# Softmax totals of layer 0: from TensorE to VectorE and GpSimd, in a kernel of two attention layers

## The chip, the cores and the metric

The kernel runs on one core of a Trainium2 chip (trn2). The core has five engines with instruction queues of their own: TensorE (PE in the profile, its weight loads PEld), VectorE (DVE), ScalarE (ACT), GpSimd (POOL) and SyncE (SP, which here only issues DMAs). Each works through its queue in program order and waits on semaphores. The metric is device time in microseconds of one execution, as the median over several runs.

## The reference, cut to what matters

The input is x of 8 batches, 512 channels and 32 x 32 positions (T = 1024), in float32. Layer 0 normalizes by groups, computes q, k and v with 8 heads of 64 channels, applies softmax attention over the positions, adds, and projects. Layer 1 does a second attention that mixes heads and normalizes the attention matrix.

```python
def _L0_conv_ref(x, gn_w, gn_b, qkv_w, qkv_b, proj_w, proj_b):
    ...
    qkv = jnp.einsum('oc,bct->bot', qkv_w, normed) + qkv_b[None, :, None]
    q, k, v = jnp.split(qkv, 3, axis=1)
    ...
    weight = jnp.einsum('bct,bcs->bts', q, k)
    weight = jax.nn.softmax(weight.astype(jnp.float32), axis=-1).astype(q.dtype)
    a = jnp.einsum('bts,bcs->bct', weight, v).reshape(b, c, t)
    out = jnp.einsum('oc,bct->bot', proj_w, xf + a) + proj_b[None, :, None]
    return out.reshape(b, -1, h, w)
...
x = x + _L0_conv_ref(_gn(x), ...)
x = x + _L1_conv_ref(_gn(x), ...)
return x
```

The change concerns the denominator of layer 0's softmax: for each head and each query position t, the sum of exp(weight) over the 1024 key positions s, and its reciprocal, which scales the attention's output.

## The kernel before

The order of the work on every engine is written out by hand (a manual schedule); pools only give out the buffers. Layer 0 runs batch after batch. For one batch, `attention0` works through NI = 64 steps. A step is one chunk of 128 key positions (kc, 0 to 7) for one pair of heads (hp) and one half of the 1024 queries (f); eight steps with the same hp and f are a group g, and there are 8 groups a batch.

- `scores(i)`: four matmuls of 64 x 64 x 512 make the scores of two heads, keys on the partitions and 512 queries in the free dimension, in PSUM; ScalarE writes their exponential to a tile e[i] of 128 x 1024 (pool of 7 buffers).
- `values(i)`: four matmuls add v times e[i] to the group's accumulators; after the last chunk ScalarE copies them to u[g] (two tiles, L1127).
- `sums(i)`: VectorE adds e[i] to zacc[g], seven adds a group (L1101 the first, L1103 the others). The partitions of zacc still hold different keys.
- `totals(g)`, once for two groups: TensorE multiplies zacc with a matrix of ones, which sums over the partitions (L1135), ScalarE copies the result to `row` (L1141), and two DMAs spread it over 128 partitions as zc (L1146).
- `reciprocals(g)`: VectorE adds the two halves of u (L1150), takes the reciprocal of zc (L1153), a DMA writes it to DRAM (zd, L1155), and two DMAs read it back, repeated over 64 partitions each (rzb, L1158). Two small instructions (L1163, L1167) fill a check.
- `finish(g)`: VectorE multiplies u with rzb (L1174) and adds the result to xa (L1176).

The loop takes two steps at a time: scores of i and i + 1, then values and sums of i - 2 and i - 1, then what the agenda holds for i and i + 1. For an odd g, whose last chunk is done at step i, it holds totals at i + 2, reciprocals of both groups at i + 6, and finish at i + 10 and i + 12. What is left at the loop's end is flushed after the next batch's k projection (`qk0`), ahead of its v projection (`v0`).

The same agenda puts other work between the steps: ScalarE's start of xa (L872) and sums for the next batch's normalization (L826, L832), VectorE's channel statistics of the batch before (L652, slots 4 to 15), the combinations of weights (L772 to L778, batches 0 to 2), the small steps of the next normalization (slots 43 to 47: `means` with the matmul L626, `squares` with L637, `scale`), and on SP the loads of x (L719) and of weights (L747, slots 32 and 33). After the loop VectorE combines tiles of the next input (`combine_right`, L885 to L888), which the k projection's second part (L906) reads.

Of the kernel before, what the change touches and what calls it, by code (L numbers as in the profile page):

```python
# [9 lines left out]
F32 = mybir.dt.float32  # L10
I32 = mybir.dt.int32
AF = mybir.ActivationFunctionType
ALU = mybir.AluOpType
AX = mybir.AxisListType
# [4 lines left out]
P = 128  # L19
# [448 lines left out]
def tile_two_attention_layers(  # L468
# [19 lines left out]
    nc = tc.nc  # L488
    B, C, T = x_d.shape
# [4 lines left out]
    FB = 512  # L494
# [206 lines left out]
    with ExitStack() as l0:  # L701
# [27 lines left out]
        HC = C // 2  # L729
# [21 lines left out]
        def load_blocks(which, queue=nc.sync, tag="u0"):  # L751

            t = left_tile(which, 0)
            if tag == "junk":
                a21[which] = zpool.tile([P, T], F32, tag=tag, name=f"a21_{which}", bufs=1)[
                    :, :C
                ].rearrange("p (k o) -> p k o", k=2)
            else:
                a21[which] = zpool.tile([P, 2, HC], F32, tag=tag, name=f"a21_{which}", bufs=3)
            for dst, i, j in (  # L760
                (t[:, 0], 0, 0), (t[:, 1], 0, 1), (a21[which], 1, 0), (t[:, 2], 1, 1),
            ):
                for k in range(2):
                    queue.dma_start(
                        out=dst[:, k],
                        in_=SOURCES[which][ts(2 * j + k, P), i * HC : (i + 1) * HC],
                    )
# [307 lines left out]

        def attention0(b, agenda):
            q, k, v = q_t[b], k_t[b], v_t[b]
            e, acc, u, zacc, zc, rzb = {}, {}, {}, {}, {}, {}

            def scores(i):  # L1080

# [13 lines left out]
            def sums(i):  # L1095
                g, kc = i // NG, i % NG
                if kc == 1:
                    zacc[g] = zpool.tile(
                        [P, 2, FB], F32, tag="zacc", name=f"zacc_{b}_{g}", bufs=3
                    )  # L1100
                    nc.vector.tensor_add(zacc[g], e[i - 1], e[i])  # L1101
                elif kc > 1:
                    nc.vector.tensor_add(zacc[g], zacc[g], e[i])  # L1103

            def values(i):

                g, hp, kc = i // NG, i // NG % (H // 2), i % NG
                if kc == 0:
                    acc[g] = [
                        ps_a.tile([P, FB], F32, tag=f"a{a}", name=f"a0_{b}_{g}_{a}", bufs=2 - a)  # L1110
                        for a in range(2)
                    ]
                for a in range(2):
                    rows = slice(a * D, a * D + D)
                    for m in range(2):
                        nc.tensor.matmul(  # L1116
                            acc[g][a][m * D : m * D + D], v[rows, kc, ts(2 * hp + m, D)],
                            e[i][rows, m], start=(kc == 0), stop=(kc == NG - 1),
                        )
                if kc == NG - 1:  # L1120

                    u[g] = [
                        zpool.tile([P, FB], F32, tag=f"u{a}", name=f"u_{b}_{g}_{a}", bufs=3 - a)
                        for a in range(2)
                    ]
                    for a in (1, 0):
                        nc.scalar.copy(u[g][a], acc[g][a])  # L1127

            def totals(g):

                HB = FB // 2
                z = ps_a.tile([P, FB], F32, tag="a0", name=f"z_{b}_{g}", bufs=2)
                for i in range(2):
                    for c in range(4):
                        nc.tensor.matmul(  # L1135
                            z[c * 32 : c * 32 + 32, ts(i, HB)], ones[:, :32],
                            zacc[g - 1 + i][:, c // 2, ts(c % 2, HB)],
                            start=True, stop=True, tile_position=(0, c * 32),
                        )
                row = zpool.tile([P, FB], F32, tag="row", name=f"row0_{b}_{g}", bufs=1)  # L1140
                nc.scalar.copy(row, z)  # L1141
                for i in range(2):
                    t = zc[g - 1 + i] = stat.tile(
                        [P, T // P], F32, tag="zc", name=f"zc_{b}_{g - 1 + i}", bufs=4
                    )
                    nc.sync.dma_start(out=t, in_=row[0::32, ts(i, HB)])  # L1146

            def reciprocals(g):

                nc.vector.tensor_add(u[g][0], u[g][0], u[g][1])  # L1150
                zs = zc[g]
                rz = stat.tile([P, T // P], F32, tag="rz0", name=f"rz_{b}_{g}")
                nc.vector.reciprocal(rz, zs)  # L1153
                zd = dram.tile([2, FB], F32, tag=f"zd0_{b}_{g}", name=f"zd0_{b}_{g}")
                nc.sync.dma_start(out=zd, in_=rz)  # L1155
                rzb[g] = zpool.tile([P, FB], F32, tag="rzb", name=f"rzb_{b}_{g}")
                for m in range(2):
                    nc.sync.dma_start(  # L1158
                        out=rzb[g][m * D : m * D + D], in_=zd[m].partition_broadcast(D)
                    )  # L1160
                col = b * H + g
                junk = stat.tile([P, T // P], F32, tag="junk0", name=f"junkz_{b}_{g}")
                nc.vector.tensor_scalar(  # L1163
                    junk, zs, 1.0, 0.0, ALU.mult, ALU.add, accum_out=chk[:, 1, col : col + 1]
                )
                r2 = stat.tile([P, T // P], F32, tag="r20", name=f"r2_{b}_{g}")
                nc.vector.scalar_tensor_tensor(  # L1167
                    r2, rz, 1.0 / RZ_MAX, rz, ALU.mult, ALU.mult,
                    accum_out=chk[:, 0, col : col + 1],
                )  # L1170

            def finish(g):
                hp, f = g % (H // 2), g // (H // 2)
                nc.vector.tensor_mul(u[g][0], u[g][0], rzb[g])  # L1174
                dst = xa_t[b][:, hp, ts(f, FB)]
                nc.vector.tensor_add(dst, dst, u[g][0])  # L1176


            for i in range(0, NI + 2, 2):
                if i < NI:  # L1180
                    scores(i)
                    scores(i + 1)
                if i >= 2:
                    for w in (i - 2, i - 1):
                        values(w)
                        sums(w)
                    if (i - 1) % NG == NG - 1:
                        g = (i - 1) // NG
                        if g % 2:
                            agenda.at(i + 2, lambda g=g: totals(g))  # L1190
                            for j in range(2):
                                agenda.at(i + 6, lambda g=g - 1 + j: reciprocals(g))
                                agenda.at(i + 10 + 2 * j, lambda g=g - 1 + j: finish(g))
                agenda.run(i)
                agenda.run(i + 1)

# [927 lines left out]
```

## Time and profile before

| | us |
|---|---|
| median of 3 runs | 3935.7 (3933.7 to 3948.0) |
| the profiled execution: its own time | 3948.0 |
| its span, first to last instruction | 3946.2 |
| TensorE busy over the span | 3871.6 (98%) |
| VectorE | 2736.6 (69%) |
| ScalarE | 1966.8 (50%) |
| GpSimd | 207.4 (5%) |
| layer 0's stretch from 95 to 1750 us: TensorE busy | 1649.2 of 1655 |
| the same stretch: VectorE, ScalarE, GpSimd | 1064.1, 801.7, 0.0 |
| granted TensorE clock | 0.998 |

In the lines of groups, the columns are line, engine, operation, output and inputs by name, shapes and count, then the total busy time, the mean of one in ns, and the idle time of the engine just before them with what ended it. In the timeline they are start and length in us, engine, line, operation and count; idle time before it stands in brackets. Matmul records overlap, so the spacing of their starts says more than their length.

### The profile page before, as it was taken

To read this page: it belongs to the slowest core of one execution; us is meant where nothing else is said; L and a number is where in the kernel's file an instruction comes from. 1 tells how busy PE (TensorE), PEld (TensorE's weight loads), DVE (VectorE), ACT (ScalarE), POOL (GpSimd) and SP (SyncE) were. 2 spreads that over 40 slices of the span, in tenths; PEclk is the share of its full clock that TensorE was granted. 3 is DMA by queue.
4 is the path that set the end of the run, shared out by engine and by line. 5 is a ranking of instruction groups with operands and counts; after the bars stand their busy time and mean duration, and the time that the engine had idled before them with its cause. 6 is when DMAs were issued, how large, how long until landed. Compare 5 with 4: busy or idle time off the path is not lost. (4 is left out here: it accounts for less than half of the span.)

```text
span 3946.2 us, 95344 instructions
## 1 busy us (share of the span) xinstructions
PE 3871.6 (98%) x41868; PEld 1822.3 (46%) x41868; DVE 2736.6 (69%) x3713; ACT 1966.8 (50%) x2400; POOL 207.4 (5%) x210
## 2 busy tenths in 40 slices
PE   8999999999999999999999999999999999999998
PEld 4353535344353535344554544545545545445454
DVE  4747476665758474756867958859768678678597
ACT  1726354453627172534725717528447257176275
POOL 0000000000000000000110100201101102002010
PEclk9999999999999999999999999999999999999999
DMA  3313131212121121216947839749559479297395
GB/s 120 120 53 116 49 116 43 84 35 77 55 75 66 64 73 52 87 46 168 221 135 190 230 97 229 191 128 239 167 149 228 142 177 223 97 227 204 114 228 146
DMA packets 249593, 519.09 MB, mean 132 GB/s; under 512 B 51024, under 2 KB 58192, under 8 KB 242512
## 3 DMA queue, kind: packets, MB, share of 16 engines
q1 hardware_dynamic: 241984, 500.08, 44.7%
q0 software_dynamic: 7184, 12.81, 1.6%
q8 instruction: 331, 5.42, 0.6%
q14 instruction: 94, 0.77, 0.1%
HBM read 197.16 MB, written 46.92 MB: 62 GB/s over the span
## 5 line engine op out<-in xcount | busy, mean ns | idle before, releaser
L1712 DVE STREAM_TRANSPOSE et<-e 128x2048 f32<-128x2048 f32 x256 | 589.5, 2303 | 133.5 <-ACT e L1697 132.5
L1742 PEld LDWEIGHTS a<-et,v 128*64 128x64 f32 x16384 | 506.4, 138 | 294.0 <-issue 268.5
L1726 DVE BATCH_NORM_STATS2 bn<-e 128x6 f32<-128x512 f32 x1024 | 635.0, 680 | 0.0
L1093 ACT ACTIVATE e<-s 128x1024 f32<-128x1024 f32 x512 | 497.1, 1026 | 232.8 <-PE s L1088 232.7
L1659 ACT COPY raw<-s 128x1024 f32<-128x1024 f32 x480 | 470.2, 1018 | 218.9 <-PE s L1647 192.5
L1697 ACT ACTIVATE e<-m 128x1024 f32<-128x1024 f32 x512 | 496.2, 1021 | 157.4 <-PE m L1684 55.1
L1742 PE MATMUL a<-et,v 128*64 128x64 f32 x16384 | 554.7, 224 | 8.7 <-issue 6.2
L1103 DVE TENSOR_TENSOR zacc<-zacc,e 128x1024 f32<-128x1024 f32 x384 | 468.8, 1221 | 124.6 <-ACT e L1093 100.5
L1647 PE MATMUL s<-k,q 64*64 64x512 f32 x4096 | 515.6, 606 | 6.9 <-DVE q L1506 3.2
L1088 PE MATMUL s<-q,k 64*64 64x512 f32 x4096 | 490.3, 594 | 2.3 <-ACT e L1093 2.3
L1116 PE MATMUL a<-e,v 64*64 64x512 f32 x4096 | 484.1, 589 | 0.0
L1684 PE MATMUL m<-re,wmix 32*32 32x512 f32 x8192 | 312.8, 599 | 17.8 <-DMA re<-raw 14.4
L1116 PEld LDWEIGHTS a<-e,v 64*64 64x64 f32 x4096 | 156.6, 133 | 282.8 <-issue 282.3
L1088 PEld LDWEIGHTS s<-q,k 64*64 64x64 f32 x4096 | 146.4, 133 | 284.2 <-issue 217.8
L1647 PEld LDWEIGHTS s<-k,q 64*64 64x64 f32 x4096 | 128.0, 132 | 222.5 <-issue 90.5
L1790 POOL DMA_DIRECT2D zd<-rz x96 | 52.3, 550 | 3390.0 <-DMA y<-x 1868.5
L1466 PE MATMUL pv<-wv,y 128*128 128x512 f32 x480 | 216.0, 603 | 0.0
L1758 ACT COPY q<-a 64x256 f32<-64x256 f32 x256 | 93.8, 367 | 136.4 <-PE a L1742 134.5
L1466 PEld LDWEIGHTS pv<-wv,y 128*128 128x128 f32 x480 | 89.3, 191 | 120.9 <-issue 107.5
L1684 PEld LDWEIGHTS m<-re,wmix 32*32 32x32 f32 x8192 | 69.3, 103 | 163.2 <-ACT raw L1659 71.7
L1472 DVE COPY v<-pv 128x512 f32<-128x512 f32 x30 | 20.7, 690 | 159.7 <-ACT v L1472 80.3
L906 PE MATMUL pv_p<-left_v,tmp 128*128 128x256 f32 x512 | 115.0, 380 | 3.3 <-DVE tmp L935 3.3
(318 smaller groups left out, 3859.5 us busy)
## 6 DMA issues: line engine op xcount, KB each, us to landing
re<-raw SPq DMA_DIRECT2D x1024, 256.0 KB
left_q<-left_q SPq DMA_DIRECT2D x17, 1792.0 KB
left_p<-left_p SPq DMA_DIRECT2D x17, 1792.0 KB
left_k<-left_k SPq DMA_DIRECT2D x10, 1792.0 KB
x<-in_x_dram SPq DMA_DIRECT2D x32, 512.0 KB
rzb<-zd SPq DMA_DIRECT2D x128, 128.0 KB
x<-x SPq DMA_DIRECT2D x64, 256.0 KB
y<-x SPq DMA_DIRECT2D x32, 512.0 KB
```

The costliest lines, as they stand in the source:

```text
L1088: nc.tensor.matmul(ps[c * D : c * D + D, m], k[r, hp, k0 : k0 + D], q[r, hp, ts(f, FB)], start=True, stop=True,)
L1093: nc.scalar.activation(e[i], ps, AF.Exp, scale=S0 * S0)
L1103: nc.vector.tensor_add(zacc[g], zacc[g], e[i])
L1116: nc.tensor.matmul(acc[g][a][m * D : m * D + D], v[rows, kc, ts(2 * hp + m, D)], e[i][rows, m], start=(kc == 0), stop=(kc == NG - 1),)
L1466: nc.tensor.matmul(ps[:, m], y_t[b][:, c, ts(2 * i + m, P)], w[:, c], start=(c == 0), stop=(c == NCC - 1),)
L1647: nc.tensor.matmul(ps[c * D : c * D + D, m], qo_t[b][r, p, hp, ts(c, D)], k_t[b][r, hp, ts(kh, FB)], start=True, stop=True,)
L1659: nc.scalar.copy(dst, ps)
L1684: nc.tensor.matmul(ps[a // 2][c * 32 : c * 32 + 32, a % 2].rearrange("p (r h k) -> p h r k", r=2, h=2), wmix[rows].rearrange("p g i -> p ( ...
L1697: nc.scalar.activation(e[:, :, 2 * h : 2 * h + 2].rearrange("p r a k -> p a r k"), ps[h].rearrange("p a (r k) -> p a r k", r=2), AF.Exp,)
L1712: nc.vector.transpose(self.et[p, u].rearrange("p kb (r st a) g q -> p st kb r (a g q)", r=2, st=2)[:, st], self.e[p, s].rearrange("p r a ( ...
L1726: nc.vector.bn_stats(self.bn[n][:, p % 2, s, a], e[:, :, a].rearrange("p r k -> p k r"))
L1742: nc.tensor.matmul(acc[two * D : two * D + D, s].rearrange("p (x q) -> p x q", q=4), v_t[b][:, kb, ts(g, D)], et[:, kb, :, g], start=(kb = ...
```

## The change

`sums`: the first three chunks of each group are added by GpSimd into a new tile zpart (two instructions); VectorE starts its own sum at chunk 4 with e[3] + e[4], adds chunks 5 and 6, then zpart, then chunk 7 (five adds). `totals` is now made for every group, without TensorE and ScalarE: VectorE transposes zacc in blocks of 32 x 32 and sums runs of 32 columns, once for each head, and transposes the small result again; four DMAs bring the four partition blocks of it side by side as zc. `reciprocals` first adds these four parts, and works on 32 x 32 instead of 128 x 8. The agenda has totals at i + 2, reciprocals at i + 8 and finish at i + 12 for every group. Buffer counts: a21 and u0 2 instead of 3, zacc 2 instead of 3.

```diff
@@ -756,7 +756,7 @@
                     :, :C
                 ].rearrange("p (k o) -> p k o", k=2)
             else:
-                a21[which] = zpool.tile([P, 2, HC], F32, tag=tag, name=f"a21_{which}", bufs=3)
+                a21[which] = zpool.tile([P, 2, HC], F32, tag=tag, name=f"a21_{which}")
             for dst, i, j in (
                 (t[:, 0], 0, 0), (t[:, 1], 0, 1), (a21[which], 1, 0), (t[:, 2], 1, 1),
             ):
@@ -1075,7 +1075,7 @@
 
         def attention0(b, agenda):
             q, k, v = q_t[b], k_t[b], v_t[b]
-            e, acc, u, zacc, zc, rzb = {}, {}, {}, {}, {}, {}
+            e, acc, u, zacc, zpart, zc, rzb = {}, {}, {}, {}, {}, {}, {}
 
             def scores(i):
 
@@ -1095,12 +1095,19 @@
             def sums(i):
                 g, kc = i // NG, i % NG
                 if kc == 1:
-                    zacc[g] = zpool.tile(
-                        [P, 2, FB], F32, tag="zacc", name=f"zacc_{b}_{g}", bufs=3
+                    zpart[g] = zpool.tile(
+                        [P, 2, FB], F32, tag="zpart", name=f"zpart_{b}_{g}", bufs=1
                     )
+                    nc.gpsimd.tensor_add(zpart[g], e[i - 1], e[i])
+                elif kc == 2:
+                    nc.gpsimd.tensor_add(zpart[g], zpart[g], e[i])
+                elif kc == 4:
+                    zacc[g] = zpool.tile([P, 2, FB], F32, tag="zacc", name=f"zacc_{b}_{g}")
                     nc.vector.tensor_add(zacc[g], e[i - 1], e[i])
-                elif kc > 1:
+                elif kc > 4:
                     nc.vector.tensor_add(zacc[g], zacc[g], e[i])
+                    if kc == NG - 2:
+                        nc.vector.tensor_add(zacc[g], zacc[g], zpart[g])
 
             def values(i):
 
@@ -1120,7 +1127,7 @@
                 if kc == NG - 1:
 
                     u[g] = [
-                        zpool.tile([P, FB], F32, tag=f"u{a}", name=f"u_{b}_{g}_{a}", bufs=3 - a)
+                        zpool.tile([P, FB], F32, tag=f"u{a}", name=f"u_{b}_{g}_{a}")
                         for a in range(2)
                     ]
                     for a in (1, 0):
@@ -1128,45 +1135,43 @@
 
             def totals(g):
 
-                HB = FB // 2
-                z = ps_a.tile([P, FB], F32, tag="a0", name=f"z_{b}_{g}", bufs=2)
-                for i in range(2):
-                    for c in range(4):
-                        nc.tensor.matmul(
-                            z[c * 32 : c * 32 + 32, ts(i, HB)], ones[:, :32],
-                            zacc[g - 1 + i][:, c // 2, ts(c % 2, HB)],
-                            start=True, stop=True, tile_position=(0, c * 32),
-                        )
-                row = zpool.tile([P, FB], F32, tag="row", name=f"row0_{b}_{g}", bufs=1)
-                nc.scalar.copy(row, z)
-                for i in range(2):
-                    t = zc[g - 1 + i] = stat.tile(
-                        [P, T // P], F32, tag="zc", name=f"zc_{b}_{g - 1 + i}", bufs=4
+                HN = FB // 32
+                pz = stat.tile([P, 2, HN], F32, tag="pz", name=f"pz_{b}_{g}")
+                for m in range(2):
+                    zt = zpool.tile([P, FB], F32, tag="zt", name=f"zt_{b}_{g}_{m}", bufs=1)
+                    nc.vector.transpose(zt, zacc[g][:, m])
+                    nc.vector.reduce_sum(
+                        pz[:, m], zt.rearrange("p (n i) -> p n i", i=32), axis=AX.X
                     )
-                    nc.sync.dma_start(out=t, in_=row[0::32, ts(i, HB)])
+                pt = stat.tile([P, 32], F32, tag="pt", name=f"pt_{b}_{g}")
+                nc.vector.transpose(pt, pz.rearrange("p m n -> p (m n)"))
+                zc[g] = stat.tile([32, 4, 32], F32, tag="zc", name=f"zc_{b}_{g}")
+                for c in range(4):
+                    nc.sync.dma_start(out=zc[g][:, c], in_=pt[c * 32 : c * 32 + 32])
 
             def reciprocals(g):
 
                 nc.vector.tensor_add(u[g][0], u[g][0], u[g][1])
-                zs = zc[g]
-                rz = stat.tile([P, T // P], F32, tag="rz0", name=f"rz_{b}_{g}")
+                zs = stat.tile([32, 32], F32, tag="zs0", name=f"zs_{b}_{g}")
+                nc.vector.reduce_sum(zs, zc[g].rearrange("p c j -> p j c"), axis=AX.X)
+                rz = stat.tile([32, 32], F32, tag="rz0", name=f"rz_{b}_{g}")
                 nc.vector.reciprocal(rz, zs)
                 zd = dram.tile([2, FB], F32, tag=f"zd0_{b}_{g}", name=f"zd0_{b}_{g}")
-                nc.sync.dma_start(out=zd, in_=rz)
+                nc.sync.dma_start(out=zd.rearrange("m (n j) -> (m n) j", j=32), in_=rz)
                 rzb[g] = zpool.tile([P, FB], F32, tag="rzb", name=f"rzb_{b}_{g}")
                 for m in range(2):
                     nc.sync.dma_start(
                         out=rzb[g][m * D : m * D + D], in_=zd[m].partition_broadcast(D)
                     )
                 col = b * H + g
-                junk = stat.tile([P, T // P], F32, tag="junk0", name=f"junkz_{b}_{g}")
+                junk = stat.tile([32, 32], F32, tag="junk0", name=f"junkz_{b}_{g}")
                 nc.vector.tensor_scalar(
-                    junk, zs, 1.0, 0.0, ALU.mult, ALU.add, accum_out=chk[:, 1, col : col + 1]
+                    junk, zs, 1.0, 0.0, ALU.mult, ALU.add, accum_out=chk[:32, 1, col : col + 1]
                 )
-                r2 = stat.tile([P, T // P], F32, tag="r20", name=f"r2_{b}_{g}")
+                r2 = stat.tile([32, 32], F32, tag="r20", name=f"r2_{b}_{g}")
                 nc.vector.scalar_tensor_tensor(
                     r2, rz, 1.0 / RZ_MAX, rz, ALU.mult, ALU.mult,
-                    accum_out=chk[:, 0, col : col + 1],
+                    accum_out=chk[:32, 0, col : col + 1],
                 )
 
             def finish(g):
@@ -1186,11 +1191,9 @@
                         sums(w)
                     if (i - 1) % NG == NG - 1:
                         g = (i - 1) // NG
-                        if g % 2:
-                            agenda.at(i + 2, lambda g=g: totals(g))
-                            for j in range(2):
-                                agenda.at(i + 6, lambda g=g - 1 + j: reciprocals(g))
-                                agenda.at(i + 10 + 2 * j, lambda g=g - 1 + j: finish(g))
+                        agenda.at(i + 2, lambda g=g: totals(g))
+                        agenda.at(i + 8, lambda g=g: reciprocals(g))
+                        agenda.at(i + 12, lambda g=g: finish(g))
                 agenda.run(i)
                 agenda.run(i + 1)
```

## The prediction

> **What bounds the kernel now.** I read the page's busy shares, then the windows of one batch of layer 0, its timeline, the groups by line and the waits. Over the attention loop of batch 1 (columns: stretch, its length, busy time of PE, PEld, DVE, ACT, POOL with instruction counts, clock, DMA share, GB/s):
>
> ```profile
> 310.50:420.50 110.00, 109.71 (x1036) 38.16 (x1036) 89.47 (x146) 86.09 (x104) 0.00 (x0) 1.00 0.29 101
> ```
>
> TensorE has no idle time (0.3 us); VectorE is next with 89.5 of 110 us; GpSimd does nothing. So a microsecond taken from TensorE is a microsecond gained, as long as VectorE, which serves it in program order, keeps up. The timeline around one totals step:
>
> ```profile
> 342.19 1.07 PE L1135 MATMUL z<-zacc,ones 128*32 128x256 f32 x16
> 343.19 1.95 PE L1088 MATMUL s<-q,k 64*64 64x512 f32 x16
> 343.33 0.59 ACT L1141 COPY row<-z 128x512 f32<-128x512 f32 x1 [1.52 <-PE z L1135]
> ```
>
> The totals hold TensorE for 1.0 us. Two such steps with nothing special between them start 28.64 us apart (129.01 and 157.65). Without a totals step the loop advances by one block of 16 records (two chunks' scores, or values) in 1.716 us (starts at 348.39, 350.11, 351.83, 353.54), so 16 blocks are 27.46 us and the totals cost up to 1.18 us. I take 1.1 us. A group (8 key chunks) lasts 8 x 1.716 = 13.73 us without totals.
>
> **What the change takes from TensorE.** Each batch has four totals steps, three inside the loop and one behind the next batch's k projection. Three in the loop: 3 x 1.1 = 3.3 us a batch. ScalarE's row copy goes too (0.59 us each), worth nothing on the path: ScalarE is busy 86 of 110 us and waits for scores. The PSUM buffer of z is no wait today (0.6 us in all before L1116 that another engine ended), and the smaller buffer counts for u, zacc and a21 add none: in the changed order each is freed a group or more before its reuse.
>
> **What VectorE gets.** The rows, from the groups by line:
>
> ```profile
> L1103 DVE TENSOR_TENSOR zacc<-zacc,e 128x1024 f32<-128x1024 f32 x384 | 468.8, 1221 | 124.6 <-ACT e L1093 100.5 <-DVE zacc L1103 1.4 <-ACT row L1141 0.5
> L1712 DVE STREAM_TRANSPOSE et<-e 128x2048 f32<-128x2048 f32 x256 | 589.5, 2303 | 133.5 <-ACT e L1697 132.5
> L566 DVE TENSOR_REDUCE sel<-ident 128x32 f32<-128x128 f32 x1 | 0.4, 359 | 0.0
> L1829 POOL TENSOR_TENSOR q<-q,rzb 128x1024 f32<-128x1024 f32 x24 | 56.6, 2358 | 165.5 <-DMA rzb<-zd 130.9 <-ACT raw L1659 19.7 <-PE a L1742 8.2
> L1366 POOL TENSOR_TENSOR right<-y 128x1024 f32<-128x1024 f32 x14 | 34.0, 2431 | 58.5 <-ACT e L1697 35.1 <-DMA re<-raw 23.4
> ```
>
> Per group: two of seven adds leave, -2 x 1.22 = -2.44 us. Two transpositions of 128x512 come: a quarter of 2303 is 0.58 (lower bound); adds of 1024 and 512 columns (1221 and 685 ns) show a fixed part near 0.15, which gives 0.69 (taken). Two run sums of 128x512: the nearest row of that width, the 128x512 statistics at 680 ns, gives 0.68 (taken); the small reductions (128x72 in 208, 128x128 in 280 ns) extend to 0.78. The last transposition is a small operation, 0.17. Together 2.91. The reciprocals get one reduction of exactly the form of L566 (0.36) and a 32-wide reciprocal (L1784: 320 ns against 197). So about +1.0 us a group: batch 1 would go from 89.5 to some 95 us, with one more reciprocals step inside the loop, of 106.7. Still under the period; but the order matters more than the sum.
>
> **The chain.** In the changed VectorE order one group reads: five adds (L1106, L1108, L1110), reciprocals of the group before (u add, zs, rz), this group's totals, finish of the group before (waits for rzb), then the next five adds. Today adds lie between reciprocals and finish and cover the way of rz to DRAM and back; there the adds of the first chunks have gone to GpSimd, and only the totals cover. The length of that way, quiet, behind the k projection:
>
> ```profile
> 451.81 0.20 DVE L1153 RECIPROCAL rz<-zc 128x8 f32<-128x8 f32 x1 [2.14 <-DMA zc<-row]
> 452.04 0.32 SPq L1155 DMA_DIRECT2D zd<-rz  x1
> 453.44 1.13 SPq L1158 DMA_DIRECT2D rzb<-zd  x2
> 457.01 0.69 DVE L1174 TENSOR_TENSOR u<-u,rzb 128x512 f32<-128x512 f32 x1 [3.86 <-DMA rzb<-zd]
> ...
> 462.26 1.21 DVE L935 TENSOR_TENSOR tmp<-tmp,pv_p 128x1024 f32<-128x1024 f32 x1
> ...
> 463.53 1.35 PE L906 MATMUL pv_p<-left_v,tmp 128*128 128x256 f32 x5 [0.24 <-DVE tmp L935]
> ```
>
> 5.0 us from the end of rz to the multiplication; beside weight transfers up to 8.2 (1631.08 to 1639.29). I take 5.0. The totals (four dependent steps of 0.69 + 0.1, then 0.2: 3.4 us) fit inside it. Adds that depend on one another start 1.33 us apart:
>
> ```profile
> 361.38 5.21 DVE L1103 TENSOR_TENSOR zacc<-zacc,e 128x1024 f32<-128x1024 f32 x4
> ```
>
> (5.21 - 1.22) / 3. The chain of a group is thus finish 1.34 (355.91 to 357.25), adds 4 x 1.33 + 1.14 = 6.46, u add 0.61, zs and rz 0.36 + 0.32 + 0.1, DMA 5.0: 14.2 us against TensorE's 13.73. VectorE falls behind by 0.45 us with each finish; six lie in the loop.
>
> **GpSimd beside VectorE.** The two adds take 2.36 to 2.43 us each and start when chunks 1 and 2 are ready. Their result is wanted at chunk 6, some 5 us after they can be done, and e has 7 buffers, which lets an add be about 8 us late before an exponential waits. So GpSimd itself is covered; with the cover gone it would cost what exceeds 8 us. What no row shows is a VectorE instruction with two SBUF inputs beside a GpSimd one. What is shown is one input:
>
> ```profile
> 1976.29 2.44 POOL L1366 TENSOR_TENSOR right<-y 128x1024 f32<-128x1024 f32 x1 [8.19 <-DMA re<-raw]
> 1977.39 2.30 DVE L1712 STREAM_TRANSPOSE et<-e 128x2048 f32<-128x2048 f32 x1
> ```
>
> 2.30 us is the transposition's usual time. Bounds of the cost: 0, and both adds in the chain's way, 4.8 us a group. The second add mostly falls in the totals, which are one-input work like this row; the first begins when the last adds and the u add are due, and an instruction that meets a 2.4 us add at a random point would wait 1.2. I take 1.2 us a group. The Trainium skill (SBUF — State Buffer, section "Who interferes with whom") speaks against the change: a VectorE instruction with two SBUF inputs and a GpSimd one that reads SBUF exclude each other, the later one waiting out the whole instruction; by that the price would lie between 2.4 and 4.8 us a group, and the sum below at +130 to +245 us. No run here shows it yet.
>
> **Sum for a batch.** Lateness of VectorE: 1.0 from the first groups (four channel statistics of 1.4 us each fall between their adds; my estimate, 0.5 to 2), 6 x (0.45 + 1.2) = 9.9, and 2.9 for the normalization's small steps, which lie between adds (388.26 to 388.92, and 391.38 to 394.54, less 0.95 of slack before chunk 6): 13.8 us. TensorE pays it at its own in-order points: the matmul that waits for gs_m (L626, now behind a totals step on VectorE), a late e, and the k projection, whose cover is:
>
> ```profile
> 425.76 1.23 DVE L886 TENSOR_TENSOR tmp<-n,tmp 128x1024 f32<-128x1024 f32 x1
> 430.95 1.45 PE L906 MATMUL pk_p<-tmp,left_k 128*128 128x512 f32 x3
> ```
>
> 4.0 us between them today, less 1.8 for the reciprocals now ahead of L885: 2.2. Stall 13.8 - 2.2 = 11.6 us. Behind the k projection z's 1.1 us go, but the last group's totals follow L962 on VectorE: from 449.07, totals 3.4, four DMA issues 0.6 apart and 1.85 to land 3.65, zs and rz 0.8, DMA 5.0, finish 1.34: 463.2, against 462.26 today, and TensorE already waits there (0.24). Net +0.8. Each group's other zc DMAs have 8 us until they are read; SP has no other work then, except a weight load ahead of some.
>
> Per batch 11.6 - 3.3 + 0.8 = +9.1 us, times 8 = **+73 us**. The profiled execution took 3948.0 (span 3946.2 and 1.8 around it), 12.3 over the median of the runs; on the median, 3935.7 + 73 = **4009 us**. Layer 1 is unchanged and keeps its time.
>
> **Rivals.** (A) Both GpSimd adds stand in the chain: 6 x 5.25 + 3.9 - 2.2 - 3.3 + 0.8 = +30.7 a batch, 4181. For it: late VectorE adds drift into GpSimd's time; against: the totals leave GpSimd a free stretch. (B) No cost beside GpSimd: 6 x 0.45 + 3.9 - 2.2 - 2.5 = +1.9 a batch, 3951. For it: the undisturbed transposition. (C) The other side, faster: the way to DRAM and back gets shorter, since rz leaves as 32 packets of 128 bytes where 128 of 32 go today. From 4.5 us on the chain is under 13.73, VectorE recovers, and the saving of 3.3 less 0.8 stays: -20 us, 3916, or 3909 if the end of the batch keeps pace too. Against it: most of the 5.0 us are two landings, not packets. That the change does not do what it says I can exclude: in the changed order the z rows are gone and each group has two GpSimd adds.
>
> **How the numbers follow.** Forecast 0.40, own range 3980 to 4066 (0.6 to 2.4 us a group beside GpSimd); A 0.17, B 0.23, C 0.20. About 0.5%, 20 us, is what a measurement of this kernel tells from no change. C gives 0.15 faster and 0.05 same; B 0.02, 0.13 and 0.08 slower; the rest is slower: 0.17, 0.18, 0.65. The range reaches from inside C (3912) to A at three quarters of its price (6 x 4.05: +188, 4124).
>
> **What would show it.** L1179 (u times rzb) idle for rzb in most groups, about 1 to 2 us; L1108 longer than 1.23 us or idle while a GpSimd add runs; TensorE idle before L626 and in the k projection by DVE, about 90 us in layer 0; layer 1 equal within 5 us. Wrong if TensorE stays without gaps in the loop (then C), or if VectorE's adds stay at 1.22 us with no idle time beside GpSimd (then B).

## The result, and the profile after

| | before | after |
|---|---|---|
| median, same chip (6 runs each) | 3941.1 us | 4089.0 us |
| ratio, 95% interval | | 1.0377 (1.0365 to 1.039) |
| span of the profiled execution | 3946.2 | 4092.9 |
| first transposition of layer 1 (a mark for the end of layer 0) | 1832.6 | 1985.8 |
| from there to the end of the span | 2113.6 | 2107.1 |

The change costs 147.9 us, twice the 73 forecast and outside the forecast's own range (3980 to 4066), and all of it lies in layer 0: its end comes 153.2 us later, and what follows is 6.5 us shorter.

The page of after, its line of busy time and its row of granted clocks (tenths of full speed, 40 slices):

```profile
PE 3883.7 (95%) x41356; PEld 1824.4 (45%) x41356; DVE 2975.7 (73%) x3969; ACT 1950.9 (48%) x2368; POOL 557.0 (14%) x338
...
PEclk9999898999999999999999999999999999999999
```

TensorE is busy for 12 us more than before although the totals' matmuls (34.3 us of rows at L1135) are gone: some of its matmuls have become slower (the part on the prediction has their lines). The windows of after show the attention loop of batch 1 (the stretch that took 110.00 us before) and what lies inside it:

```profile
322.50:456.50 134.00, 118.57 (x1036) 40.13 (x1034) 120.36 (x175) 86.47 (x102) 44.93 (x16) 0.95 0.26 90
...
400.00:412.00 12.00, 4.15 (x40) 1.22 (x32) 11.37 (x15) 3.26 (x5) 5.00 (x2) 0.88 0.34 136
412.00:420.00 8.00, 3.73 (x18) 1.55 (x22) 6.12 (x15) 1.02 (x1) 1.05 (x1) 0.50 0.12 38
```

The loop now takes 134 us, and VectorE (third figure) is busy for 120.4 us of it, more than TensorE: 89.5 before, some 95 in the forecast. In the middle of it TensorE stands still for 12 us and then runs at a granted clock of 0.50. What it waited for in layer 0 (waits of after: line, what ended them, total us, times, longest):

```profile
PE pm L626 <- DVE gs_m L624: 81.9, 7, 12.8
PE pk_p L906 <- DVE tmp L886: 24.8, 7, 3.6
PE pv_p L906 <- DVE tmp L935: 15.8, 7, 3.2
PE s L1088 <- ACT e L1093: 8.6, 13, 2.8
```

All waits of TensorE from 90 to 1870 us add up to 143.3 us (5.8 before, from 90 to 1760 us), and 122.5 of them are the first three places, those at which it needs something from VectorE. So VectorE is late; its timeline over one group of after, and GpSimd's, show why:

```profile
389.32 1.23 DVE L1110 TENSOR_TENSOR zacc<-zacc,zpart 128x1024 f32<-128x1024 f32 x1
390.65 1.23 DVE L1108 TENSOR_TENSOR zacc<-zacc,e 128x1024 f32<-128x1024 f32 x1
391.80 2.86 DVE L1154 TENSOR_TENSOR u<-u,u 128x512 f32<-128x512 f32 x1
394.58 0.36 DVE L1156 TENSOR_REDUCE zs<-zc 32x32 f32<-32x128 f32 x1
394.98 0.34 DVE L1158 RECIPROCAL rz<-zs 32x32 f32<-32x32 f32 x1
395.25 0.12 DVE L1168 TENSOR_SCALAR_CACHE_REDUCE junkz<-zs 32x32 f32<-32x32 f32 x1
...
395.35 1.59 DVE L1172 SCALAR_TENSOR_TENSOR r<-rz 32x32 f32<-32x32 f32 x1
...
400.23 0.69 DVE L1179 TENSOR_TENSOR u<-u,rzb 128x512 f32<-128x512 f32 x1 [0.22 <-DMA rzb<-zd]
```

```profile
390.69 3.42 POOL L1101 TENSOR_TENSOR zpart<-e,e 128x1024 f32<-128x1024 f32 x1 [10.03 <-DVE zacc L1110]
394.19 2.71 POOL L1103 TENSOR_TENSOR zpart<-zpart,e 128x1024 f32<-128x1024 f32 x1
```

GpSimd's first add is released when VectorE has read zpart (L1110) and starts beside an add of VectorE, which keeps its 1.23 us; GpSimd's takes 3.42 instead of 2.37. The u add of VectorE (L1154), issued next, takes 2.86 us where it took 0.69, and ends at 394.66, 0.55 us after GpSimd's first add (394.11): it looks like a wait for that add, and then the u add's own work. The reductions and the reciprocal beside the second one are not lengthened, but the check with two inputs (L1172), 0.17 us before, takes 1.59 and ends with it (396.9). A long instruction on a page of times can thus be a wait that no wait view shows. The groups of layer 0 say that this is the rule. The u add and the check of before, then the groups of after:

```profile
L1150 DVE TENSOR_TENSOR u<-u,u 128x512 f32<-128x512 f32 x64 | 43.9, 685 | 0.0
L1167 DVE SCALAR_TENSOR_TENSOR r<-rz 128x8 f32<-128x8 f32 x64 | 10.7, 167 | 0.0
```

```profile
L1154 DVE TENSOR_TENSOR u<-u,u 128x512 f32<-128x512 f32 x64 | 134.7, 2105 | 0.0
L1142 DVE STREAM_TRANSPOSE zt<-zacc 128x512 f32<-128x512 f32 x128 | 90.2, 704 | 2.5
L1143 DVE TENSOR_REDUCE pz<-zt 128x16 f32<-128x512 f32 x128 | 87.8, 686 | 4.4
L1172 DVE SCALAR_TENSOR_TENSOR r<-rz 32x32 f32<-32x32 f32 x64 | 77.8, 1216 | 0.0
```

The u add means 2105 ns (685 before), the check 1216 (167 before): (1.42 + 1.05) x 64 = 158 us of VectorE's time. The single u adds leave nothing between: 42 of the 64 start while a GpSimd add runs and last 2.83 to 2.86 us, whether that add was issued 0.1 or 1.2 us earlier; the other 22 meet none and last 0.68 to 0.69. From one finish to the next (384.01, 400.23, 416.32 us) a group takes 16.2 us on VectorE, against TensorE's 13.73.

### The profile page after: what moved, and what is told of

It reads as the page before. It is cut to its first block, busy times and chain, and to the rows that moved or that the text cites. A ratio compares the mean times of both kernels' runs of the same rounds, so it can differ in the third digit from the quotient of the medians.

```text
span 4092.9 us, 95103 instructions
## 1 busy us (share of the span) xinstructions
PE 3883.7 (95%) x41356; PEld 1824.4 (45%) x41356; DVE 2975.7 (73%) x3969; ACT 1950.9 (48%) x2368; POOL 557.0 (14%) x338
## 5 line engine op out<-in xcount | busy, mean ns | idle before, releaser
L1088 PE MATMUL s<-q,k 64*64 64x512 f32 x4096 | 503.2, 607 | 8.6 <-ACT e L1093 8.6
L1123 PE MATMUL a<-e,v 64*64 64x512 f32 x4096 | 488.9, 594 | 0.0
L1101 POOL TENSOR_TENSOR zpart<-e,e 128x1024 f32<-128x1024 f32 x64 | 187.9, 2935 | 1462.9 <-ACT e L1093 1191.3
L1108 DVE TENSOR_TENSOR zacc<-zacc,e 128x1024 f32<-128x1024 f32 x192 | 234.5, 1221 | 20.9 <-ACT e L1093 4.5
L1103 POOL TENSOR_TENSOR zpart<-zpart,e 128x1024 f32<-128x1024 f32 x64 | 161.8, 2528 | 29.3 <-ACT e L1093 25.9
L906 PE MATMUL pk_p<-tmp,left_k 128*128 128x512 f32 x256 | 127.4, 656 | 24.8 <-DVE tmp L886 24.8
```

The costliest lines, as they stand in the source:

```text
L1088: nc.tensor.matmul(ps[c * D : c * D + D, m], k[r, hp, k0 : k0 + D], q[r, hp, ts(f, FB)], start=True, stop=True,)
L1123: nc.tensor.matmul(acc[g][a][m * D : m * D + D], v[rows, kc, ts(2 * hp + m, D)], e[i][rows, m], start=(kc == 0), stop=(kc == NG - 1),)
```

## The experiments

Each is the changed kernel (e5: the kernel before) with the edit whose main lines are shown, timed in three rounds (e11: five) beside the kernel before on the same chip.

| run | what | us | ratio to before |
|---|---|---|---|
| after | | 4089.0 | 1.0377 (1.0365 to 1.039) |
| e1_clear | u add and checks away from GpSimd's adds | 3986.1 | 1.0118 (1.0094 to 1.0142) |
| e2_late_finish | finish two slots later | 4053.4 | 1.0283 (1.0266 to 1.03) |
| e3_clear_late | both | 3968.9 | 1.0067 (1.0049 to 1.0084) |
| e4_zpart2 | two buffers for zpart | 4132.0 | 1.0484 (1.0467 to 1.0502) |
| e5_gpsimd_alone | GpSimd's adds without VectorE's totals | 3972.0 | 1.0073 (1.0056 to 1.0089) |
| e6_vector_alone | VectorE's totals without GpSimd's adds | 3996.6 | 1.0137 (1.0119 to 1.0155) |
| e7_early_gs_m | copy to gs_m earlier | 4077.1 | 1.0347 (1.0326 to 1.0368) |
| e8_clear_late_early | e3, copy to gs_m and last totals earlier | 3918.7 | 0.9947 (0.993 to 0.9963) |
| e9_arranged_no_gpsimd | e8 without GpSimd | 3954.0 | 1.0037 (1.0022 to 1.0053) |
| e10_e8_and_gs | e8, normalization's steps moved once more | 3952.7 | 1.0025 (1.0015 to 1.0035) |
| e11_filler | idle time before L626 filled with matmuls | 4100.3 | 1.0404 (1.0379 to 1.0429) |

**e1_clear: the instructions that met GpSimd's adds are moved out of their way.** `reciprocals` is split in three; the u add goes two slots ahead, the two checks six slots behind.

```diff
+                        agenda.at(i + 6, lambda g=g: halves(g))
                         agenda.at(i + 8, lambda g=g: reciprocals(g))
                         agenda.at(i + 12, lambda g=g: finish(g))
+                        agenda.at(i + 14, lambda g=g: checks(g))
```

> Only the order on VectorE changes: the u add goes to slot i + 6 and the two check instructions to i + 14, away from the stretch in which GpSimd adds; finish stays at i + 12. In the changed kernel the u add takes 2.11 us on average instead of 0.69 and the product of the reciprocals 1.22 instead of 0.17, and a group's cycle on VectorE is 16.2 us. Theory (waits beside GpSimd are the larger part): both go back to under 0.75 and 0.25 us, the cycle falls to 14.2 to 14.6, bound by the way of rz to DRAM and back; time 3950 to 3985 us against 3941 before and 4089 changed. Rival (VectorE's own work or the in-order rzb wait sets the cycle): the waits come back in other instructions, time over 4040 us.

3986.1, a microsecond above the theory's range and far from the rival's: 103 us of the 148 are gone. The groups of e1:

```profile
L1154 DVE TENSOR_TENSOR u<-u,u 128x512 f32<-128x512 f32 x64 | 43.2, 676 | 0.0
L1182 DVE SCALAR_TENSOR_TENSOR r<-rz 32x32 f32<-32x32 f32 x64 | 11.2, 175 | 0.0
```

Not one instruction was taken away, so what these two instructions paid beside GpSimd is what those 103 us were, together with what the lateness brought on TensorE. No run moved one of the two alone. Now the way of rz to DRAM and back, which the long u add had kept out of sight, ends the chain: e1's timeline has

```profile
377.89 0.34 DVE L1163 RECIPROCAL rz<-zs 32x32 f32<-32x32 f32 x1
...
384.15 0.69 DVE L1189 TENSOR_TENSOR u<-u,rzb 128x512 f32<-128x512 f32 x1 [2.92 <-DMA rzb<-zd]
```

5.9 us from the end of rz; all such waits in layer 0 come to 117.8 us (52 of them; 59.8 in after). Finishes start at 354.76, 369.09, 384.15 and 398.33: 14.2 to 15.1 us a group, what the prediction had for a chain without any waiting beside GpSimd (14.2).

**e2_late_finish and e3_clear_late: the finish two slots later, so that two more adds cover the way of rz;** e2 by itself, e3 on top of e1.

```diff
-                        agenda.at(i + 12, lambda g=g: finish(g))
+                        agenda.at(i + 14, lambda g=g: finish(g))
```

> Only finish goes from i + 12 to i + 14, behind two adds of the next group, so that rzb has landed long before it is read. Theory of the prediction (the 5.0 us way of rz is a term of the chain): the cycle loses what the totals do not cover, time under 4040 us. Rival (waits beside GpSimd hold VectorE for as long as the way takes, so that it is hidden anyway; rzb is waited for only 59.8 us in all in the changed kernel): 4070 to 4100 us.

> Both of the other edits: u add at i + 6, finish and checks at i + 14. Without waits beside GpSimd and without the rzb wait VectorE's own work is about 12.9 us a group, under TensorE's 13.73. Theory: VectorE keeps up except in the normalization's small steps, TensorE's saving shows; 3910 to 3945 us. Rival (VectorE's own work is too much): over 3965 us.

e2 gave 4053.4: between the two, 36 us better than after. In e2 the wait for rzb is left only in the flush (8 times, 41.3 us), yet u add (1937 ns) and check (1242) are as long as in after. Where two things each hold the chain, taking one away gives part of it. e3 gave 3968.9: 17 better than e1, but still slower than before: 24 above the theory's range and inside the rival's. The rival's reason (VectorE's own work is too much) does not fit the trace, though: the groups take 13.2 to 14.0 us on VectorE where no other work lies between, so the loop itself nearly keeps pace. What is left in e3's waits:

```profile
PE pm L626 <- DVE gs_m L624: 22.8, 8, 5.4
PE pv_p L906 <- DVE tmp L935: 18.3, 7, 3.7
```

The first is a copy of 128x4 that VectorE reaches only behind a totals step; the second is the flush, where totals, four DMAs, reciprocals, the way of rz and finish of the last group come in a row ahead of L935.

**e4_zpart2: a second buffer for zpart** (and one in place of two for zacc, to make room), so that GpSimd need not wait for VectorE's read.

```diff
-                        [P, 2, FB], F32, tag="zpart", name=f"zpart_{b}_{g}", bufs=1
+                        [P, 2, FB], F32, tag="zpart", name=f"zpart_{b}_{g}", bufs=2
```

> zpart gets two buffers (zacc one, to make room; its sums start at chunk 4, after the totals that read the buffer). In the changed kernel GpSimd's first add often starts right when VectorE has read zpart (252.3 us of waits), just ahead of the u add. If that single buffer makes the collision, time falls to 4000 us or under and the u add is back under 1 us. If GpSimd's adds exclude VectorE's two-input instructions wherever they fall, the waits move to VectorE's adds of e and the time stays at 4060 to 4110 us.

4132.0, slower than after by 43, and 22 above the range expected even if GpSimd's adds exclude VectorE wherever they fall. GpSimd's first add is no longer held back by zpart (all 64 now wait for e alone); it starts earlier and meets the adds of e as well. Groups of e4:

```profile
L1108 DVE TENSOR_TENSOR zacc<-zacc,e 128x1024 f32<-128x1024 f32 x192 | 301.9, 1572 | 20.2 <-ACT e L1093 3.2 <-DVE zacc L1106 0.5 <-DVE mv L838 0.4
L1110 DVE TENSOR_TENSOR zacc<-zacc,zpart 128x1024 f32<-128x1024 f32 x64 | 100.2, 1566 | 7.4 <-DVE zacc L1108 0.9
...
L1154 DVE TENSOR_TENSOR u<-u,u 128x512 f32<-128x512 f32 x63 | 75.6, 1200 | 0.0
```

L1108 and L1110 rose from 1.22 us to 1.57, and the u add fell to 1.20: the price goes to whichever two-input instruction stands there. In the order of the change the single buffer had been a help, since it kept VectorE's adds clear.

**e5_gpsimd_alone and e6_vector_alone: each half of the change by itself.** e5 is the kernel before with `sums` of the change; e6 is the change with `sums` of before (all seven adds on VectorE).

> Only the GpSimd adds of the change; the totals stay on TensorE, with the order of before. VectorE loses 16 us of adds a batch and gets at most 4.8 us a group of waiting beside GpSimd, 38 us a batch; it had 17 us of 107 free. Theory (the exclusion costs time only where VectorE has none to spare): VectorE instructions beside the GpSimd adds are lengthened here as well (some group means of two-input work over 1.4 us where they were 1.22 or 0.69), yet the time is 3925 to 3965. Rival (a GpSimd add beside VectorE costs its time wherever it stands, about 100 us): 4000 or more.

> Only the totals on VectorE; all seven adds stay there, GpSimd does nothing, order as in the change. VectorE per group: 7 adds at 1.22 and gaps of 0.1, totals 2.95, u add 0.68, zs and rz 0.70, finish 1.38, checks 0.5: 15.5 us against TensorE's 13.73. Theory (what GpSimd takes off VectorE it gives back in waits): 4040 to 4090, within 50 us of the changed kernel. Rival (GpSimd's two adds are a help worth their 2.44 us a group): 4150 or more.

e5 gave 3972.0, 7 above the range of the theory and 28 below the rival's: the exclusion is there (in e5 the multiplication with rzb means 1466 ns, the add to xa 949, both 0.69 before), and VectorE's slack covers part of it; TensorE waits 31.5 us in all, 18.0 of them at L626. e6 gave 3996.6, below both. VectorE does two adds more a group there and still needs only 14.6 us (finishes at 354.40, 369.12, 383.68, 398.30) where after needs 16.2. So GpSimd's two adds, meant to take 2.44 us off VectorE's group, cost it 1.6 net, and 92 us in the kernel. Two things are in this price. One is the wait beside GpSimd. The other is cover: in e6 the first adds of the next group lie between reciprocals and finish, and in the loop VectorE waits for rzb only twice (0.16 and 0.73 us); with these adds on GpSimd only the totals are left there, and in e1, where the wait beside GpSimd is gone, the wait for rzb holds most groups. My count of 15.5 for e6 was too high: several instructions on VectorE overlap their predecessors by some 0.1 us.

**e7_early_gs_m: the copy for L626 earlier.** Is the place where TensorE waits the cause, or only where it pays?

```diff
+            agenda.at(slot + 20, gs.copy)
             agenda.at(slot + 23, gs.means)
```

> The changed kernel, with the copy to gs_m (L624) made three slots earlier, ahead of a totals step on VectorE; its matmul stays where it is. Theory (VectorE's lateness is the cause, the matmul behind gs_m only the place where it is paid): the waits before L626 shrink from 81.9 us to under 60, those at the k projection grow, and the time stays at 4060 to 4095. Rival (the place is the cause): 4020 or less.

4077.1, in the theory's range: the waits at L626's matmul fall from 81.9 to 36.1, and those at the next small matmul (L637) rise from 3.1 to 19.4; those at the k projection, which were to grow, fall from 24.8 to 21.3. The time falls by 12 us, for 46 us of wait removed at L626 and 32 us in all of layer 0 (151.4 to 119.7 from 95 us on), while TensorE is busy 12.7 us longer for the same work; part of the gain may be VectorE's own, whose u add means 1736 ns there. With VectorE late by 2.5 us a group, TensorE pays most of it elsewhere.

**e8_clear_late_early: e3 with both of its left-over waits treated.** In e3 VectorE is no longer late, so the same edit should be worth its full price there.

```diff
+            agenda.at(slot + 20, gs.copy)
             agenda.at(slot + 23, gs.means)
...
                 combine_right(f"{b + 1}", n_t[b + 1])
+                ag.run(slot)
                 qk0(b + 1, "k")
```

(`slot` is NI + 2 there: the last group's totals. They now run while VectorE waits for the k projection.)

> The u add apart from the reciprocals, the checks and the finish two slots later (as in e3), and in addition the copy to gs_m three slots earlier and the last group's totals ahead of the k projection's matmuls instead of behind them. Theory (e3's remaining loss is the 22.8 us before L626 and the 18.3 us before the flush's matmul, and half clock after them): 3905 to 3940, both waits under 8 us in all. Rival (what is left comes from GpSimd beside VectorE all the same): 3955 or more.

3918.7, ratio 0.9947 (0.993 to 0.9963): 50 us less than e3, a little faster than before, and 170 less than the change as made. The two places wait 6.2 us and nothing, all waits of TensorE 20 us (53.7 in e3, both up to 1870 us). Finishes at 345.90, 359.07 and 372.69: 13.2 and 13.6 us, under TensorE's 13.73.

**e9_arranged_no_gpsimd: does GpSimd help in this order?** e8 with all adds on VectorE.

> e8 with all seven adds on VectorE and none on GpSimd. VectorE per group by the rows of e6: 15.2 us or so (7 adds of 1.22 and gaps, totals 2.95, u add 0.68, zs and rz 0.70, finish 1.38, checks 0.3) against e8's two adds less and what its GpSimd adds still lengthen. Theory (a GpSimd add pays only where nothing that excludes it is due; in e8 it mostly is so): 3935 to 3975, slower than e8 by 20 to 55. Rival (GpSimd's adds are worth nothing even there): 3915 or less.

3954.0: slower than e8 by 35. In the order of the change GpSimd's adds cost 92 us, in this one they bring 35. What differs is what stands on VectorE while they run (in e8 the reduction, the reciprocal and the totals, and the first add of e, which still pays 0.25 us a group: L1111 of e8 means 1466 ns), and that the later finish leaves the way of rz covered with or without the two adds (44 us of waits for rzb in e8, 43 in e9, nearly all in the flush). No run separates the two shares.

**e10_e8_and_gs: the last small waits.** The copy to gs_m earlier still (in e8 it takes 2.3 us, beside a GpSimd add), the matmul of gs_sq one slot later, and with it the `scale` step one slot later.

```diff
-            agenda.at(slot + 20, gs.copy)
+            agenda.at(slot + 10, gs.copy)
...
-            agenda.at(slot + 27, scale)
+            agenda.at(slot + 26, gs.spread)
+            agenda.at(slot + 28, scale)
```

> e8 with the copy to gs_m ten slots earlier still (it met a GpSimd add and took 2.3 us) and the matmul of gs_sq one slot later. Theory (the waits of 6.2 us before L630 and 5.6 before L641 are paid in full): 3903 to 3914. Rival (they are covered elsewhere, or come back at the k projection): 3915 to 3922, as e8.

3952.7: both expectations missed, 34 slower than e8. The waits aimed at did shrink (1.6 and 4.7 us left), but ScalarE's normalization, in its queue ahead of the exponentials, needs nn, the last result of `scale`. e10's timelines of ScalarE and VectorE:

```profile
402.68 1.24 ACT L879 ACTIVATE n<-x,nn,scale 128x1024 f32<-128x1024 f32 x1 [6.06 <-DVE nn L823]
```

```profile
397.45 0.15 DVE L810 COPY gvar<-pv 128x4 f32<-128x4 f32 x1
397.64 2.12 DVE L812 TENSOR_SCALAR gve<-gvar 128x4 f32<-128x4 f32 x1
```

ScalarE stands for 6.06 us (seven times, 31.3 us), the exponentials behind it are late, and TensorE waits 33.5 us for e (2.9 in e8). In its new slot the `scale` step also begins beside a GpSimd add (396.35 to 399.74), and a step of 128x4 takes 2.12 us instead of 0.17. That the later `scale` step is the cause is read from this trace; no run made the three moves of e10 one by one.

**e11_filler: what the idle time before L626 and the slow clock behind it are worth.** Nine matmuls into the bank that L626 overwrites.

```diff
             self.pm = self.psum(f"pm_{self.nm}")
+            if fill is not None:
+                for _ in range(9):
+                    nc.tensor.matmul(self.pm, gavg, fill(), start=True, stop=True)
```

> The changed kernel with nine extra matmuls (128x128 by 128x512, into the bank that L626 writes, and overwritten by it) ahead of L626 in layer 0: about 8 us of work (0.44 us a record, 18 records) inside a wait of 12. If the fall of TensorE's clock after that wait stands on the path: the wait shrinks to about 4 us each, the blocks behind it last 1.72 us in place of 3.47 and 3.13, and the time falls by up to 3.2 us x 7 = 22, to 4060 to 4075, although work was added. Rival (VectorE sets the pace of the loop, so half-speed blocks only fill time that TensorE would wait for it later): 4080 to 4095, with the clock whole behind L626 and the waits later in the batch longer by about as much.

4100.3, above both ranges (5 us over the rival's); the interval of its ratio overlaps that of after. TensorE did 8.0 us more work a batch, 56 in seven, and its waits fell from 143.3 to 94.1 us: that the time moved by only 11 us shows that VectorE, not TensorE, sets the pace of after's loop, as the rival has it. The clock part failed on both sides, since a wait of 5.1 us was still enough for half speed. After's timeline behind its wait, and e11's:

```profile
416.27 0.59 PE L626 MATMUL pm<-gs_m,gavg 128*128 128x4 f32 x2 [12.12 <-DVE gs_m L624]
416.78 3.69 PE L1088 MATMUL s<-q,k 64*64 64x512 f32 x16
420.25 3.20 PE L1123 MATMUL a<-e,v 64*64 64x512 f32 x16
...
423.70 1.95 PE L1088 MATMUL s<-q,k 64*64 64x512 f32 x16
```

```profile
417.54 0.59 PE L629 MATMUL pm<-gs_m,gavg 128*128 128x4 f32 x2 [5.11 <-DVE gs_m L624]
418.06 3.69 PE L1092 MATMUL s<-q,k 64*64 64x512 f32 x16
421.52 2.42 PE L1127 MATMUL a<-e,v 64*64 64x512 f32 x16
```

The blocks take 3.47 and 3.13 us (starts 416.78, 420.25, 423.38) instead of 1.716, and 3.46 and 2.36 in e11. So the run does not separate how much of the slow clock stands on the path at this place.

## Why the prediction was right in direction and wrong in size

The direction, the mechanism (VectorE's chain longer than TensorE's group, paid at in-order points) and the places held; the size was half of what came. The step that failed is one term of the sum, the wait beside GpSimd: 1.2 us a group were taken, and 2.15 came in the chain (2.47 of VectorE's time).

- **What TensorE saves** (3.3 us a batch in the loop, some 26 in all): right. The 34.3 us of z are gone, and they show as a gain once nothing is late: e8 is 25 us under before.
- **VectorE's new work**: right. Transposition 0.69 forecast and 0.704 measured, run sum 0.68 and 0.686, the small one 0.17 and 0.21, the reduction 0.36 and 0.36.
- **The quiet chain of 14.2 us**: right by e1 (14.2 to 15.1), with a way of rz of 5.9 us in the group shown where 5.0 was taken.
- **The failing step: "I take 1.2 us a group" beside GpSimd.** It cost 2.47 us of VectorE's time a group. Of that the check's part fell into the way of rz, which runs anyway (in the group above rz is finished at 395.32 and rzb is there at 400.23, 4.9 us later, with no idle time on VectorE but 0.22); the u add's 2.15 us in the loop are the chain's. 14.2 + 2.15 = 16.35 against the measured 16.2. How the check and the u add share the price is this reading of the trace; e1 moved both. The 1.2 rested on an instruction that meets a GpSimd add at a random point. But the meeting is not at a random point: GpSimd's add, issued beside an add of VectorE, waits for that one and goes ahead just as the u add is due, so the u add waits out nearly all of it (2.15 of 2.37 us) in all 42 groups where they meet. That GpSimd's adds start when chunks 1 and 2 are ready was also wrong for 24 of the 64 first adds: they stood until VectorE had read zpart, of which there is one buffer (L1110), one add ahead of the u add. The row that the prediction leaned on, a transposition beside a GpSimd add at its usual 2.30 us, was of one input, and it said nothing of two. The prediction had itself written that the first add begins when the last adds and the u add are due.
- The Trainium skill (SBUF — State Buffer, "Who interferes with whom") says that the later of the two waits out the whole of the earlier one. The runs agree: 3.42 us for GpSimd's add when it comes second, 2.86 for the u add when it does, and reductions and transpositions untouched. The value taken lay below the bound that the prediction had worked out from this rule, 2.4 us a group; 2.47 was measured.
- **Lateness and stall**: with 2.15 in place of 1.2 the prediction's own sum has 6 x (0.45 + 2.15) + 3.9 - 2.2 = 17.3 us a batch of waiting, 5.7 more than its 11.6; measured are 143.3 / 8 = 17.9, or 15.9 without the flush's 15.8 us, which the sum has apart. By the sum this accounts for 46 of the 75 us that were missing.
- **Not in the sum: what a wait leaves behind on TensorE.** Behind the waits in the k and v projections the matmuls of 128x512 and 128x256 mean 665 and 407 ns (592 and 381 before): 113.4 - 98.4 and 110.6 - 100.8, 25 us more for the same work (the lines stand below this list). In the loop the matmuls of scores and values take 17.7 us more (503.2 + 488.9 against 490.3 + 484.1). In e8, without the waits, the first two are back at 595 and 379, and the last at 493.9 + 486.0. This is read from rows, and from e8 taking 50 us off e3 where 34 us of waits went; no run tried the clock alone at this place, so how much of it stands on the path is open.
- The Trainium skill (TensorE: Matmul & The Clock Gate, Part 1) has the clock at half rate after about one idle window of 3.4 us, and full after about one busy one. The 0.50 behind the 12 us wait agrees; that the slow blocks go on for 6.6 us there is longer, and waits shorter than such a window were followed by half the clock as well: behind the wait of 2.55 us in the v projection of after, 0.50 was granted from 504.8 to 508.2 us.
- **The flush**: +0.8 us a batch forecast, too little: TensorE waits 15.8 / 7 = 2.3 there, where it waited 3.3 in all before (0.24 in the batch shown).
- **Rivals.** A (both adds in the chain) named the right place and too large a price: the adds of e kept 1.22 us, because GpSimd's add came second to them. B (no cost beside GpSimd, 3951) has its condition nearly met in e1, which ends at 3986; the 35 us between are put down to the longer way of rz and the flush, and not separated. e6, without GpSimd but with seven adds on VectorE, ends at 3997. C, faster because VectorE recovers, needed a shorter way to DRAM, which did not come. e8 comes near its price of 3916 by another road: there the way is covered.
- **What would show it**: the wait for rzb was forecast at 1 to 2 us in most groups; it is mostly 0.2 to 1.1 in the loop, since the check's wait had taken its place, and appears when that goes (e1). L1108 was named as the add to be lengthened; it was the u add behind it. The sign named for B (VectorE's adds stay at 1.22 us, without idle time) thus came nearly true, and B did not hold: the sign looked at one line, and the price was on another. TensorE's waits at L626 and in the k projection were forecast at about 90 us and came to 106.7. Layer 1 differs by 6.5 us where 5 were allowed.

The lines of the k projection's second part, before and after:

```profile
L906 PE MATMUL pk_p<-tmp,left_k 128*128 128x512 f32 x224 | 98.4, 592 | 0.0
```

```profile
L906 PE MATMUL pk_p<-tmp,left_k 128*128 128x512 f32 x224 | 113.4, 665 | 24.8 <-DVE tmp L886 24.8
```

## What to carry to other kernels

Before work goes to GpSimd, write out which two-input VectorE instructions will be issued while it runs, and put reductions, transpositions or PSUM reads there instead: the same two adds cost 92 us in one order and bring 35 in another. Ask also what the work that leaves had covered: here the adds had covered the way of rz to DRAM and back. When an engine is late, moving the place where others wait for it gains little (12 us for 46 us of wait at that place in e7); make its chain shorter than the period first, then the edit pays (50 us in e8, together with the earlier totals). And follow every small step to its last reader on every queue: one slot's delay of a 128x4 step stopped ScalarE, and TensorE behind it, for 34 us (e10).

## What the runs showed of the hardware that was not expected

- Some small one-input instructions wait as well: the copy of 128x4 at L624 means 2323 ns in e8 (0.13 at 416.08 in after, where GpSimd is idle), and a step of 128x4 with constants took 2.12 us in e10 (0.17 before). Beside GpSimd's adds a reduction, a reciprocal and a transposition of 128x512 kept their times, and so did a copy of 128x4 out of PSUM (L810 in e10, 0.15).
- GpSimd waits too when it comes second: 3.42 us for an add that takes 2.37 alone, issued 0.04 us after an add of VectorE of 1.23. VectorE's add, the first to start, kept its time.
- A wait of 5.1 us left TensorE at a granted clock of 0.50 (416 to 420 us of e11), and one of 2.55 us did so for 3.4 us (504.8 to 508.2 us of after).
